# One indirect table fetch, later row transpositions, routing in parts and warm-up products in a fused adapter and mixture-of-experts kernel

## Chip, cores and metric

The kernel runs on one core of one Trainium2 chip. The metric is device time in microseconds (us), the median over several runs of the whole program. A profile is one execution recorded by the hardware profiler; its span goes from the first to the last recorded instruction.

## What is computed

The input x holds 8 sequences of 256 rows with 1024 columns, 2048 rows in all. The reference, cut to its core:

```
w = weight[adapter_ids]                     # per sequence, one of 8 matrices 1024 x 1024
y = einsum('bsi,boi->bso', x, w)            # "cond"
shared = silu(y @ Sg.T) * (y @ Su.T) @ Sd.T # shared expert, inner size 1024
probs  = softmax(y @ gate_w.T)              # 16 experts
top-2, renormalised -> combine              # row by row
e_out  = (silu(y @ Wg[e].T) * (y @ Wu[e].T)) @ Wd[e].T   # inner size 256, per expert
out = x + shared + sum_e combine[:, e] * e_out
```

All is float32. The kernel splits each operand into a high part (a float32r value) and a low part (the remainder), and makes three products per pair: high by high, high by low, low by high.

## The kernel before

**Layout.** Rows are worked in 4 groups of 512 (GT), each of 4 blocks of 128 (NB). Groups 0 and 1 form a first pair and 2 and 3 a second pair for the shared expert.

**Weights.** `load_w` (L89) is the only way by which weights come in: SP issues a 512-KB load to a staging buffer (4 of them), ScalarE casts it to the high part (L80), VectorE subtracts for the low part (L81), both in a buffer `hl` of the pool `whl` (5 of them). After each load it takes one entry from the list `between` and lets that work be queued behind the load's split; this is how other work is strewn among the loads by hand. The order within each engine's queue is fixed when the program is built, by a scheduler that simulates the program and may move an instruction ahead when it finds its data ready; `issue_after` keeps an instruction behind another one on that one's engine.

**Stages.**
1. `cond(b)` (L209) multiplies sequence b by its adapter matrix: 8 weights and 2 loads of transposed x, 96 products of 512 columns (L104 to L106), results to DRAM (`y_d`, L233). The adapter's number is read by SP from `it_sb`.
2. Rows of y come back by POOL's queue (`y_block`, L347), and VectorE transposes them (L178) to the operands `raw` of the shared expert, or to `tt`.
3. The shared expert's up part uses seven half-size products in place of eight (class `Up`, L374): stages A to D for the first pair, each with weights from `sgu` and sums of weights (`sums_b`, L434, which loads two pieces of sgu by L439 and L440 into free parts of S and raw, and stores sums in `ss_d`). Their products are L425, 512 columns each.
4. `route(g, parts)` (L236) makes one group's router logits, 16 or 32 products (L242, from `rb`, the split of transposed rows), then on VectorE the softmax, the top two and each row's rank within its expert. It scatters row numbers and weights to a table in DRAM, `tab_d`, by 8 indirect stores (L333). For groups 1 to 3 its operands come from `parts_of` (L363).
5. After group 3, VectorE orders the experts by load (L782 to L817). `entries` (L660) fetches the table for a list of experts: for each, SP reads the expert's number and issues two small loads, `tb` (L670, for the row numbers) and `cr` (L671, for the weights). `places` transposes tb and adds offsets by four POOL instructions (L656), which gives the gather indices `ix`; `weights` transposes cr on TensorE (L683) and copies it to `cw` (L686). It is called for experts 0 and 1 first, then for the other 14.
6. `expert_rows` (L690) gathers an expert's rows by 8 to 10 indirect loads on POOL (L579); `transpose_rows` (L205) turns and splits them into `yte`. Meanwhile `shared_down` (L533) does the down part of the shared expert for groups 0 and 1, 384 products, adding each finished accumulator to rows of x on VectorE (L554).
7. The 16 experts follow, then the second pair's shared expert with `combine` (L558), which gathers the experts' outputs.

**Helpers at the beginning.** `constants` (L132) makes identity, triangle and index constants on POOL. `tables` (L155) loads the gate and stores an empty table; `zeros` (L168) stores zero rows from SP.

The calls around the change:

```
between[:] = [None, w[0], w[1], lambda: tables(ring), None, w[2], None, w[3]]
cond(2, ys)
...
between[:] = up.rows_work(1)
up.stage_a(0)
up.stage_a(1)
route(1, parts_of([raw[1][:, :, k * 2 * P : (k + 1) * 2 * P] for k in range(2)]))
zeros(ys)
```

Of the kernel before, what the change touches and what calls it, by code (L numbers as in the profile page):

```python
# [17 lines left out]
P = 128  # L18
B, S, H = 8, 256, 1024
T = B * S  # L20
# [3 lines left out]
G = 4  # L24
GT = T // G
# [5 lines left out]
SLOTS = T + CAP  # L31
# [6 lines left out]
def adapter_moe_kernel(ctx: ExitStack, tc: tile.TileContext, xT, x, itok, wc, gate, wgu, wd, sgu, sd, out):  # L38
# [45 lines left out]

    homes, loads, last_gather, marks = [whl], [0], [None], []
# [3 lines left out]
    def load_w(src, parts=1):  # L89
# [3 lines left out]
        for i in range(parts):  # L93
            cs = slice(i * 1024 // parts, (i + 1) * 1024 // parts)
            last_load[0] = nc.sync.dma_start(st[:, cs], src[:, cs])
            end = split(hl[:, 0, cs], hl[:, 1, cs], st[:, cs])
# [5 lines left out]

    def mm3(ps, lhs, rhs, first, last):
        nc.tensor.matmul(ps, lhs[0], rhs[0], start=first, stop=False)  # L104
        nc.tensor.matmul(ps, lhs[0], rhs[1], start=False, stop=False)  # L105
        nc.tensor.matmul(ps, lhs[1], rhs[0], start=False, stop=last)  # L106
# [4 lines left out]
    gpk = cpool.tile([P, NC * 2 * E + P], FR, tag="gpk", name="gpk")  # L111
# [3 lines left out]
    nc.sync.dma_start(it_sb, itok)  # L115

    ident = cpool.tile([2 * E, 2 * E], F32, tag="ident", name="ident")
# [9 lines left out]
    c1, c2 = (t[:, :, 1:2].bitcast(F32).rearrange("p a o -> p (a o)") for t in tid)  # L127
    msum = cpool.tile([P, E], BF, tag="msum", name="msum")
# [3 lines left out]
    def constants(ring):  # L132
        make_identity(nc, ident)
# [3 lines left out]
        nc.gpsimd.memset(ones, 1.0)  # L137
# [30 lines left out]
    def zeros(ys):  # L168
        zr = ys.tile([P, 1024], F32, tag="yr", name="zr")
        nc.gpsimd.memset(zr, 0.0)  # L170
        nc.sync.dma_start(y_d[T // P].rearrange("a p f -> p a f"), zr[:, :].rearrange("p (a f) -> p a f", a=4))
        nc.sync.dma_start(comb_d[T : T + P, :], zr[:, :E])
        nc.sync.dma_start(os_d[ZROW : ZROW + 16, :], zr[:16, :])
# [19 lines left out]
    def pair_work(tb, ys):  # L193
        tv = tt.rearrange("p k (b n) -> p (k b) n", b=4)
        r = [y_block(tb + k, ys) for k in range(2)]
        return tv, [lambda k=k: transpose_to(tv[:, :, k * P : (k + 1) * P], r[k], 4) for k in range(2)]

    def transposed_pair(tb, ys):
        tv, works = pair_work(tb, ys)
        for work in works:  # L200
            work()
        return tv


# [4 lines left out]
    def cond(b, rows):  # L209
        xt = [load_w(xT[b, :, 0, :], 2 if b == 0 else 1)]  # L210
        aid = nc.values_load(it_sb[0:1, b : b + 1], engines=(mybir.EngineType.SP,), min_val=0, max_val=NA - 1)
        yrow = [rows.tile([P, 1024], F32, tag="yrow", name=f"yrow{k}") for k in range(2)]
        for h in range(2):
            ps = [bank() for k in range(2)]
            for q in range(4):
                if h == 0 and q == 1:
                    xt.append(load_w(xT[b, :, 1, :]))
                w = load_w(wc[ds(aid, 1), h * 4 + q].rearrange("a p f -> p (a f)"), 2 if b == 0 and h == 0 and q == 0 else 1)
# [17 lines left out]
    def route(g, parts):  # L236
        lp = psm.tile([P, GT], F32, tag="sm", name="lp")
        n0 = 0
        for get, n in parts:
            for c in range(NC):  # L240
                for l in range(2):
                    nc.tensor.matmul(  # L242
                        lp[:, n0 : n0 + n],
                        gpk[:, c * 2 * E : c * 2 * E + P],
                        get(c)[l],
                        start=(c == 0 and l == 0),
                        stop=(c == NC - 1 and l == 1),
                    )
            n0 += n
# [3 lines left out]
        for k in range(NB):  # L253
            nc.tensor.transpose(lt[:, k, :], ls[: 2 * E, k * P : (k + 1) * P], ident)
# [108 lines left out]
    def parts_of(srcs):  # L363
        for src in srcs:
            t = []
            for k in range(2):
# [618 lines left out]
```

## Time and profile before

| | |
|---|---|
| median of 3 runs | 1003.71 us (998.79 to 1004.02) |
| the profiled execution's own time | 1005.67 us |
| its span | 1003.8 us |
| mean granted TensorE clock | 0.997 |
| instructions | 14185, of them 5043 products |
| moved by DMA | 252.45 MB, mean 251 GB/s |
| largest DMA queues, share of 16 engines | SP 50.5%, POOL 20.7%, ACT 4.6% |

On the page, engines are PE (TensorE's products), PEld (its weight loads), DVE (VectorE), ACT (ScalarE), POOL (GpSimd) and SP (SyncE). In the rows by slices each digit is a fortieth of the span (25 us) in tenths. A row of a timeline gives the start, the duration, the engine, the line, the operation, what is written and read, and in brackets the idle time before it and who ended it. A row of waits gives the total, the number and the longest, in us. In a chain of waits each row is a start, a length and what ran. Stages by time: the eight `cond` blocks, stages A to D and the four routings until about 362 us, `shared_down` for groups 0 and 1 until 457, the experts until 758, the second pair until 998.

### The profile page before, as it was taken

The page shows a single profiled execution, that of the slowest core. Times are in us where ns is not written, and L with a number is a line of the kernel's source. Part 1 is how long each engine was busy: PE and PEld are TensorE (multiplying, and loading weights), DVE is VectorE, ACT ScalarE, POOL GpSimd, SP SyncE. Part 2 cuts the span into 40 slices and gives each one's busy share as a digit, 9 for nine tenths or more (in the row PEclk, how much of TensorE's full clock was granted, in tenths as well). Part 3 has the DMA queues.
Part 4 walks back from the last instruction along what each step waited for, and adds up shares of the span by engine and source line. Part 5 has one row for each costly group of instructions (what it writes and reads, how often), then busy time and mean ns, then how long its engine had stood idle before and what let it go on. Part 6 is the DMA issues. An engine that isn't in the chain of part 4 may idle for free.

```text
span 1003.8 us, 14185 instructions
## 1 busy us (share of the span) xinstructions
PE 980.0 (98%) x5043; PEld 839.8 (84%) x5043; DVE 661.6 (66%) x886; ACT 531.6 (53%) x709; POOL 303.5 (30%) x312
## 2 busy tenths in 40 slices
PE   6989999999999999989999999999999999999997
PEld 5868888888788888869999999999998888888886
DVE  5567588565875886847978878878785324565531
ACT  5546466466563451316777767767665556233220
POOL 1000303000003004847885664650003442503200
PEclk9999999999999999999999999999999999999999
DMA  8988647978768133739988888888878999956931
GB/s 296 319 299 296 210 148 230 389 271 308 283 219 296 44 126 118 268 117 358 332 315 297 269 292 288 278 286 306 283 252 305 260 327 305 290 147 198 263 127 44
DMA packets 83782, 252.45 MB, mean 251 GB/s; under 512 B 13366, under 2 KB 22198, under 8 KB 83702
## 3 DMA queue, kind: packets, MB, share of 16 engines
q1 hardware_dynamic: 51526, 174.07, 50.5%
q0 software_dynamic: 19312, 60.47, 20.7%
q10 hardware_dynamic: 12864, 16.91, 4.6%
q8 instruction: 41, 0.67, 0.3%
q14 instruction: 39, 0.32, 0.1%
HBM read 203.17 MB, written 48.25 MB: 250 GB/s over the span
## 4 chain that ended last, share of the span: by engine, by line
PE 84%; DMA 6%; POOL 3%; issue 3%; DVE 2%; SPq 1%; ACT 1%; ACTq 0%; POOLq 0%; DVEq 0%
PE acc L425 28%; PE acc L105 18%; PE acc L106 18%; PE acc L104 17%; DMA st<-wc 3%; PE acc L647 2%; POOL yg L579 2%; DMA y_d<-yrow 1%; DMA yr<-y_d 1%; PE lp L242 1%; DVE hl L81 1%; POOL tab_d L333 1%; ACT hl L80 1%; DMA st<-xT 1%; SPq L670 0%
## 5 line engine op out<-in xcount | busy, mean ns | idle before, releaser
L81 DVE TENSOR_TENSOR hl<-st,hl 128x1024 fp32r<-128x1024 f32 (+1 forms) x254 | 305.0, 1209 | 176.8 <-ACT hl L80 175.7
L80 ACT CAST hl<-st 128x1024 fp32r<-128x1024 f32 (+1 forms) x254 | 262.9, 1042 | 203.6 <-PE acc L106 80.4
L425 PE MATMUL acc<-op,hl 128*128 128x512 f32 x1056 | 242.6, 390 | 0.5 <-DVE hl L81 0.5
L425 PEld LDWEIGHTS acc<-op,hl 128*128 128x128 f32 x1056 | 197.5, 188 | 41.7 <-DVE hl L81 1.0
L579 POOL DMA_INDIRECT yg<-y_d,ix x128 | 162.7, 1271 | 57.9 <-issue 34.1
L104 PE MATMUL acc<-yte,hl 128*128 128x256 f32 (+6 forms) x512 | 147.4, 288 | 0.0
L106 PE MATMUL acc<-yte,hl 128*128 128x256 f32 (+6 forms) x512 | 147.3, 288 | 0.0
L105 PE MATMUL acc<-yte,hl 128*128 128x256 f32 (+6 forms) x512 | 146.9, 287 | 0.0
L105 PE MATMUL acc<-hl 128*128 128x512 f32 x256 | 101.0, 394 | 2.8 <-DVE hl L81 2.8
L104 PE MATMUL acc<-hl,ht 128*128 128x512 f32 x256 | 99.6, 392 | 1.4 <-DVE acc L554 1.4
L105 PE MATMUL acc<-hl,ht 128*128 128x512 f32 x256 | 100.6, 393 | 0.0
L104 PE MATMUL acc<-hl 128*128 128x512 f32 x256 | 92.1, 395 | 8.6 <-ACT hl L80 8.6
L106 PE MATMUL acc<-hl 128*128 128x512 f32 x256 | 100.4, 392 | 0.0
L106 PE MATMUL acc<-hl,ht 128*128 128x512 f32 x256 | 100.0, 392 | 0.0
L105 PEld LDWEIGHTS acc<-yte,hl 128*128 128x128 f32 x512 | 96.4, 188 | 0.6
L104 PEld LDWEIGHTS acc<-yte,hl 128*128 128x128 f32 x512 | 96.4, 188 | 0.6
L106 PEld LDWEIGHTS acc<-yte,hl 128*128 128x128 f32 x512 | 96.2, 188 | 0.0
L347 POOL DMA_DIRECT2D yr<-y_d x24 | 13.3, 552 | 249.5 <-DMA y_d<-yrow 138.4
L425 PE MATMUL acc<-op,shl 128*128 128x512 f32 x288 | 66.7, 389 | 0.0
L104 PEld LDWEIGHTS acc<-hl 128*128 128x128 f32 x256 | 48.3, 190 | 19.4 <-ACT hl L80 9.5
L425 PEld LDWEIGHTS acc<-op,shl 128*128 128x128 f32 x288 | 54.1, 188 | 11.2
L333 POOL DMA_INDIRECT tab_d<-tid,sli x32 | 35.1, 1098 | 87.7 <-DVE ranks L326 78.9
(191 smaller groups left out, 1330.5 us busy)
## 6 DMA issues: line engine op xcount, KB each, us to landing
st<-wgu SPq DMA_DIRECT2D x64, 512.0 KB
st<-wc SPq DMA_DIRECT2D x63, 512.0 KB
st<-sd SPq DMA_DIRECT2D x32, 512.0 KB
st<-wd SPq DMA_DIRECT2D x32, 512.0 KB
os_d<-o SPq DMA_DIRECT2D x32, 512.0 KB
yr<-y_d POOLq DMA_DIRECT2D x24, 512.0 KB, 6.4
st<-sgu SPq DMA_DIRECT2D x24, 512.0 KB
st<-ss_d SPq DMA_DIRECT2D x20, 512.0 KB
```

Source lines behind the costliest of these rows:

```text
L80: nc.scalar.copy(hi, src)
L81: return nc.vector.tensor_tensor(lo, src, hi.bitcast(F32), op=ALU.subtract).ins
L104: nc.tensor.matmul(ps, lhs[0], rhs[0], start=first, stop=False)
L105: nc.tensor.matmul(ps, lhs[0], rhs[1], start=False, stop=False)
L106: nc.tensor.matmul(ps, lhs[1], rhs[0], start=False, stop=last)
L242: nc.tensor.matmul(lp[:, n0 : n0 + n], gpk[:, c * 2 * E : c * 2 * E + P], get(c)[l], start=(c == 0 and l == 0), stop=(c == NC - 1 and l == 1),
L333: i = nc.gpsimd.indirect_dma_start(out=tab_d[:, :], out_offset=bass.IndirectOffsetOnAxis(ap=sli[:, k : k + 1], axis=0), in_=tid[r][:, tb, ...
L347: nc.gpsimd.dma_start(r, y_d[tb].rearrange("a (i t) f -> (a i) (t f)", t=4))
L425: nc.tensor.matmul(ps, lhs[x], rhs[y], start=(first and c == 0 and i == 0), stop=(c == 3 and i == 2), skip_group_check=True)
L579: last_gather[0] = nc.gpsimd.indirect_dma_start(out=r[:, t * 256 : (t + 1) * 256], out_offset=None, in_=y_d.rearrange("k a p f -> (k a p) f"),
L647: nc.tensor.matmul(ps, a3[:, fi, :], w[fi][:, l, hs], start=(fi == 0 and l == 0), stop=(fi == 1 and l == 1))
```

## The change

**Table.** The table's stride per expert, SLOTS, becomes a multiple of 320 (ENTRIES), so that the first 320 entries of an expert are one row of a view. `entries` no longer loops: VectorE works out on each partition p the row of the expert that is p modulo 16 in the order (`column`, four instructions), one indirect load on POOL fetches these rows to all 128 partitions, one VectorE transposition and one addition give `ix` for all experts. `weights` runs once, held behind the last product queued then.

**Order.** The transpositions of the first expert's rows are queued after loads 4, 6 and 7 of the second `shared_down` (before: 1, 3 and 5). `parts_of` is replaced by `half_part`, and routing is queued through `between` among the loads of stage A (group 1) and of cond 6 and stage C (group 2); group 3 keeps its place. The first loads are issued in a given order (`load_first`), the second half of x one weight later; gate and empty table, and the first two pieces of sgu, are held behind the loads issued by then. `sums` is split into a list of instructions, called in the same place.

**Beginning and end.** Twelve products of constants are queued first on TensorE. `zeros` stores from POOL. The last four output stores go by ACT. `sq` moves from a row buffer of `ys` to `mid`. `G = 4` is renamed GN.

```diff
+ENTRIES = -(-CAP // 32) * 32
+SLOTS = -(-(T + CAP) // ENTRIES) * ENTRIES
...
+    def load_first(xsrc, wsrc):
+        pieces = []
+        for src in (xsrc, wsrc):
+            st = wst.tile([P, 1024], F32, tag="wst", name="st")
+            loads[0] += 1
+            pieces.append((src, st, homes[loads[0] % len(homes)].tile([P, 2, 1024], FR, tag="whl", name="hl")))
+        for k, i in ((0, 0), (1, 0), (1, 1), (0, 1)):
+            src, st, hl = pieces[k]
+            cs = slice(i * 512, i * 512 + 512)
+            with tc.issue_after(last_load[0].ins):
+                last_load[0] = nc.sync.dma_start(st[:, cs], src()[:, cs])
+            split(hl[:, 0, cs], hl[:, 1, cs], st[:, cs])
+        return pieces[0][2], pieces[1][2]
...
+    def after_loads(work):
+        def later():
+            with tc.issue_after(last_load[0].ins):
+                work()
+        return later
...
+    nc.gpsimd.memset(ones, 1.0)
+    warm = psm.tile([P, 4, P], F32, tag="sm", name="warm")
+    for k in range(12):
+        nc.tensor.matmul(warm, ones, ones[:, :].rearrange("p (o n) -> p o n", o=1).to_broadcast([P, 4, P]), start=True, stop=True)
...
-        nc.sync.dma_start(y_d[T // P].rearrange("a p f -> p a f"), zr[:, :].rearrange("p (a f) -> p a f", a=4))
+        nc.gpsimd.dma_start(y_d[T // P].rearrange("a p f -> p a f"), zr[:, :].rearrange("p (a f) -> p a f", a=4))
...
-                if h == 0 and q == 1:
+                if h == 0 and q == 2:
                     xt.append(load_w(xT[b, :, 1, :]))
...
+    def half_part(lp, k, src):
+        t = []
+        for q in range(2):
+            rb = whl.tile([P, 2, 4, 2 * P], FR, tag="whl", name="rb")
+            split(rb[:, 0], rb[:, 1], src[:, 4 * q : 4 * q + 4, :])
+            t.append(rb)
+        route_part(lp, k * 2 * P, lambda c: [t[c // 4][:, l, c % 4, :] for l in range(2)], 2 * P)
+
+    def group_work(lp, g, ys):
+        tv = tt.rearrange("p k (b n) -> p (k b) n", b=4)
+        r = [y_block(g * NB + k, ys) for k in range(2)]
+        def block(k):
+            transpose_to(tv[:, :, k % 2 * P : k % 2 * P + P], r[k], 4)
+            if k < 2:
+                r.append(y_block(g * NB + k + 2, ys))
+        works = []
+        for k in range(2):
+            works += [lambda k=k: block(2 * k), lambda k=k: block(2 * k + 1), lambda k=k: half_part(lp, k, tv)]
+        return works
...
+    def entries(pool, column):
+        cr = pool.tile([P, ENTRIES, 2], F32, tag="cr", name="cr", bufs=1)
+        ib = pool.tile([P, ENTRIES // 32, 32], F32, tag="ib", name="ib", bufs=1)
+        nc.gpsimd.indirect_dma_start(
+            out=cr.rearrange("e s o -> e (s o)").bitcast(I32),
+            out_offset=None,
+            in_=tab_d.rearrange("(e s) o -> e (s o)", s=ENTRIES),
+            in_offset=bass.IndirectOffsetOnAxis(ap=column, axis=0),
+        )
+        nc.vector.transpose(ib, cr[:, :, 0].rearrange("p (t i) -> p t i", i=32))
+        nc.vector.tensor_scalar(ix, ib.rearrange("p t n -> p n t")[:, :E, :].bitcast(I32), seg[:, 0:1], None, op0=ALU.add)
...
-    between[:] = [None, w[0], w[1], lambda: tables(ring), None, w[2], None, w[3]]
+    between[:] = [None, w[0], w[1], after_loads(lambda: tables(ring)), None, w[2], None, w[3]]
...
-    between[:] = up.rows_work(1)
+    w = up.rows_work(1)
+    lp = logits()
+    part = lambda k: lambda: half_part(lp, k, raw[1][:, :, k * 2 * P : (k + 1) * 2 * P])
+    between[:] = [w[0], w[1], w[2], both(w[3], part(0)), part(1), lambda: route(1, lp)]
     up.stage_a(0)
     up.stage_a(1)
-    route(1, parts_of([raw[1][:, :, k * 2 * P : (k + 1) * 2 * P] for k in range(2)]))
+    up.stage_a(2)
     zeros(ys)
-    up.stage_a(2)
+    after_loads(lambda: up.sums_loads(0))()
...
-    between[:] = [None, None, None, w[0], None, None, w[1]]
+    lp2 = logits()
+    w = group_work(lp2, 2, ys)
+    between[:] = [None, None, None, w[0], None, None, w[1], None, None, w[2], both(*w[3:]), lambda: route(2, lp2)]
     cond(6, ys)
-    route(2, parts_of(tv if k == 0 else transposed_pair(2 * NB + k, ys) for k in (0, 2)))
...
-    places, weights = entries(pe[1], [0, 1])
-    places()
+    weights = entries(pe[1], column)
     e0 = expert_rows(pa[1], 0)
-    between[:] = [None] * 4 + [weights]
     shared_down(0, G, ring, down_rows(0, ys), xs_d)
     rs = expert_rows(pa[1], 1)
-    places, weights = entries(pe[1], range(2, E))
     yt, works = expert_yt_work(pa[1], e0)
-    between[:] = [works[0], None, works[1], places, works[2], None, weights]
+    between[:] = [None, weights, None, works[0], None, works[1], works[2]]
     shared_down(1, S_, ring, down_rows(1, ys), xs_d)
```

## Prediction

> **What bounds the kernel now.** I read the page first: its busy row, then the slices.
>
> ```profile
> PE 980.0 (98%) x5043; PEld 839.8 (84%) x5043; DVE 661.6 (66%) x886; ACT 531.6 (53%) x709; POOL 303.5 (30%) x312
> ...
> DMA  8988647978768133739988888888878999956931
> ```
>
> TensorE sets the time, but 98% flatters it. A 512-column product is recorded as lasting 390 ns although the next one starts 227 ns later, so gaps below 0.2 us look busy. I therefore went through TensorE's rows in order of time and took, for each product, the time to the next start less the median for its shape (227 ns at 512 columns, 118 at 256, 139 at 304). The medians sum to 970.5 us. Beside them stand 7.3 us before the first product, 6.7 us after the last start, and 19.3 us beyond the pace; together the span of 1003.8. The 19.3 lie at: 7.3 to 11.7 us, 2.2; 11.7 to 14.2, 1.3; 35, 0.6; 57 to 60, 2.2; 71 to 75, 2.0; 130, 0.9; 266, 2.1; 355 to 380, 0.8; 433, 1.7; 441.8 to 445.2, 3.2; 445.3 to 449, 1.6; scattered, 0.8. From 450 us on, where the experts begin, there is nothing to win. No change that leaves the products alone can go below about 984.5 of span.
>
> The list of TensorE's waits names the releasers:
>
> ```profile
> PE acc L104 <- ACT hl L80: 8.6, 3, 7.3
> PE ct L683 <- DMA cr<-tab_d: 3.0, 1, 3.0
> PE acc L105 <- DVE hl L81: 2.8, 4, 1.4
> PE acc L104 <- DVE acc L554: 1.4, 1, 1.4
> ```
>
> Then TensorE's timeline around the largest ones (start, duration, form), first the beginning:
>
> ```profile
> 10.91 0.63 PE L105 MATMUL acc<-hl 128*128 128x512 f32 x1
> 11.34 0.61 PE L106 MATMUL acc<-hl 128*128 128x512 f32 x1
> ...
> 12.02 0.39 PE L106 MATMUL acc<-hl 128*128 128x512 f32 x1
> 12.61 0.73 PE L104 MATMUL acc<-hl 128*128 128x512 f32 x2 [0.21 <-ACT hl L80]
> 13.87 0.50 PE L105 MATMUL acc<-hl 128*128 128x512 f32 x1 [0.53 <-DVE hl L81]
> 14.21 0.40 PE L106 MATMUL acc<-hl 128*128 128x512 f32 x1
> ```
>
> The first ten products start 0.43 apart, later ones 0.23. But the thirteenth starts at 12.61 because its weight is just cast, the fifteenth at 13.87 because its low part is just made: data, not pace, sets where the second group of twelve begins. And the middle:
>
> ```profile
> 441.77 0.39 PE L104 MATMUL acc<-hl,ht 128*128 128x512 f32 x1
> 445.20 0.43 PE L683 MATMUL ct<-ident,cr 16*128 16x16 f32 x3 [3.04 <-DMA cr<-tab_d]
> 445.56 0.79 PE L105 MATMUL acc<-hl,ht 128*128 128x512 f32 x1
> 446.15 0.63 PE L106 MATMUL acc<-hl,ht 128*128 128x512 f32 x1
> ```
>
> Three small transpositions of table weights stand in TensorE's queue and wait for cr. Their loads are 28 small DMAs (two for each of 14 experts), issued by SP from 431.8 to 444.1, 0.44 us each, and SP began only when POOL had zeroed cr at 431.2, behind the second expert's row gathers. After the gap the pace is halved again. The stretches confirm this (columns: length; busy time and count of PE, PEld, DVE, ACT, POOL; granted clock, DMA share, GB/s):
>
> ```profile
> 7.30:11.70 4.40, 4.37 (x10) 3.42 (x11) 1.74 (x3) 1.85 (x3) 0.00 (x0) 1.00 1.01 329
> 445.20:448.60 3.40, 3.40 (x10) 2.79 (x11) 0.32 (x2) 0.00 (x0) 2.58 (x5) 0.51 0.84 245
> ```
>
> Granted clock 0.51 goes with a 0.43 pace. At the start the row says 1.00 with the same 0.43, so I trust the pace.
>
> **Part by part.**
>
> *One table fetch.* Removed: 32 small DMAs on SP, POOL's zeroing, four POOL additions twice. So the transpositions that wait for cr find it there some 40 us early: 3.2 + 1.6 = 4.8 us. I take 4.6 (bounds 2 and 4.8, the low end if the weight products meet another wait). Added: four VectorE steps for the column, 0.2 us each by the 16-column rows, in a chain that has slack (below), and a POOL fetch of 128 rows of 2,560 B, 328 KB. It must wait for the last table scatter, issued at 393.7 and landed near 396.6, where SP's first table load started before. The nearest rows are the 128-KB row gather (5.3 us from issue to landing) and the 512-KB block read (6.4), so about 5.5. [...] Behind the waiting fetch on POOL stand only those gathers. Behind VectorE's transposition of the fetched table stand splits of weights for up to 5.5 us; ScalarE at that time waited 12.4 us for TensorE to free weight buffers, four loads of 24 products (5.4 us each) ahead, so TensorE doesn't see it.
>
> *Later row transpositions.* The wait at 433 is an accumulator bank whose addition (L554) came late, because VectorE sat before transpositions of rows that hadn't landed. They move behind later loads, using the 30 us of slack: 1.5 (0 to 1.7).
>
> *Constant products.* Twelve, 0.43 apart if slow: from about 1.1 us (their memset goes first on POOL) to 6.2, ahead of the first real one at 7.3, so free. [...] By the timeline a fast array only reaches the wait at 12.61 sooner: nothing by itself.
>
> *Order of the first loads.* What ends that wait is the second weight piece. The change puts it ahead of the second half of x, so 0.5 MB less stands in front: 1.4 us at the 360 GB/s of this stretch. I take 1.3 for both together (0 to 3.4, the two items in full).
>
> *Early loads moved.* SP issued the gate (7.5 us), the empty table (9.5) and two pieces of sgu (11.9, 13.0), and a 0.5-MB store followed at 22.5: 1.9 MB among loads running at 300 GB/s, 6 us of transfer. Sgu goes to about 150 us, where the stretch 140 to 160 has DMA 0.62 busy; gate and table to about 50. The wait at 35 goes (0.6). The one at 57, where ScalarE sat 3.7 us for x, should go too, but a chain then bites:
>
> ```profile
> 57.06 6.40 DMA y_d<-yrow
> ...
> 64.01 6.43 DMA yr<-y_d
> ...
> 71.63 1.19 DVE hl L81
> ```
>
> Store, read back, transposition, and behind it on VectorE the weight split that TensorE needs: 14.6 us from the end of the second block, whatever came before. So most of 2.2 + 2.0 moves from 57 to 71. I take 1.0 (-2 to 3.8), and charge 0.3 (0 to 1.5) for the gate's cast, which now stands in ScalarE's queue with its load issued just before.
>
> *Routing in parts.* The same 112 router products. At 266 TensorE ran into them before their operand was split; now half of them fall among later loads, with stage C's products ready beside them: 1.2 (-1 to 2.1). At 130: 0.4 (-2 to 0.9). Each half takes two of five weight buffers, as before.
>
> *Zeros on POOL, last stores on ACT.* SP waited 16.6 us for POOL's zeros, but its next load (133.9) waited for a buffer anyway; POOL is idle there, three issues at 0.55 us: 0. The last store was issued at 998.3 and landed at 1001.3; another queue changes that by -0.3 to 0.5: 0.
>
> Sum: 4.6 + 1.5 + 1.3 + 0.6 + 1.0 - 0.3 + 1.2 + 0.4 = 10.3. The profiled execution took 1005.7 for its span of 1003.8, so 995.4 for a span of 993.5; from the runs' median, 1003.7, it is 993.4. I say 993.5.
>
> **Rivals.**
>
> *Hidden anyway.* The start is held by the store-and-read chain and the routing waits only move; just the table and transposition parts count, 4.6 + 1.5: 997.6. For it: 14.6 us of chain that the change doesn't touch. Against: DMA share 0.9 to 1.0 until 60.
>
> *A wait in place of the one removed.* The fetch or a moved transposition blocks VectorE until a weight or a bank is late, 4 us, and a gap of over 3 us costs 1.6 more at half clock: about 999. For it: VectorE's queue is in order, and gathers landed late there. Against: the cover of 20 us.
>
> *Slower: router products at the head of TensorE's queue.* In group 1 the first half's split is written behind the fourth transposition, which waits for rows landed at 124.4; ready then at 128.2. If the order of the queues keeps this, TensorE arrives after one stage (106.9 + 48 products of 227 ns = 117.8) and waits 10.4, plus 1.6 for the clock: 12.0, more than all gains, 1005.4; twice, in group 2 as well, 1017. It decides from a wait over 10.3. Against: before, the same split ran at 109.9, ahead of those rows, and 11 router products stood between others without a wait.
>
> That the one fetch isn't made, or not early, is the second rival's limit: without the 4.6 it is 998.
>
> **Numbers.** Forecast 0.60, hidden anyway 0.18, wait replaced 0.12, slower 0.10. About 5 us, 0.5%, is what a measurement can tell here (the three runs span 5.2). Below 998.7 I put 0.58 of the first, 0.12 of the second, 0.03 of the third: 0.73; above 1008.7, 0.07; between, 0.20. The range runs from near the floor (984.5 + 1.9, rounded up to 987) to 1002.
>
> **What would show it.** No TensorE wait on cr, granted clock 1.00 through 440 to 450; first table index before 404; real products 0.23 apart from 7.3 us, the second group complete near 12.5; a wait near 70 still there. Wrong would be: a wait of TensorE on rb or lp over 3 us, VectorE waiting for cr with TensorE idle, or a start that gains over 5 us.

## The result and the profile after

The changed kernel is slower. Its median is 1010.64 us (1009.55 to 1013.2, 4 runs) against 1002.59 us (998.79 to 1004.02, 4 runs) on the same chip: ratio 1.0086, 95% interval 1.006 to 1.0112. Measured again in two later sets of runs, beside before each time, the ratio was 1.0077 (1.0044 to 1.0111) and 1.012 (1.0089 to 1.0152). The forecast was 993.5. Medians are over all executions; ratios leave out those in which the chip was in a slower state, so the two can differ a little.

The profiled execution took 1009.55 us, its span 1007.8. The pair of traces differs by only 4.0 us of span, since the profiled execution of before (1005.67) was slower than all its timed runs and that of after its fastest.

The page of after, the two rows shown of before:

```profile
PE 988.2 (98%) x5052; PEld 844.5 (84%) x5052; DVE 659.2 (65%) x887; ACT 531.3 (53%) x709; POOL 311.1 (31%) x314
...
DMA  7887837989779345587898888888878999956931
```

The busy share is again 98% and says nothing. TensorE's waits in after say more:

```profile
PE acc L127 <- DVE acc L619: 2.8, 1, 2.8
PE acc L127 <- ACT hl L82: 2.6, 1, 2.6
PE lp L269 <- ACT rb L82: 2.3, 1, 2.3
PE lp L269 <- issue: 1.9, 1, 1.9
...
PE acc L486 <- DVE X L569: 1.1, 1, 1.1
```

The wait on cr is gone, as predicted. In its place stand a wait for an accumulator's addition (L619), and one on rb, the operand of the router products. The prediction had named such a wait, if over 3 us, as a sign that it is wrong: here it is 2.3, and 0.8 on the second split of rb; in the two repeats it is 4.8 and 6.0.

I keep the prediction's measure: the start of each product less the median pace of all work before it, TensorE's **lag**. It grows where TensorE loses time. By stretches of TensorE's own work (not of the clock on the wall), in us:

| work done | lost before | lost after | gained | predicted |
|---|---|---|---|---|
| 0 to 60 | 15.3 | 11.9 | 3.4 | 2.6 with the next row |
| 60 to 110 | 0.5 | 4.3 | -3.8 | |
| 110 to 150 (group 1) | 1.3 | 6.7 | -5.4 | 0.4 |
| 150 to 300 (group 2) | 1.9 | 1.3 | 0.7 | 1.2 |
| 300 to 400 | 0.8 | 2.1 | -1.3 | 0 |
| 400 to 430 (table) | 6.4 | 4.6 | 1.8 | 6.1 |
| 430 to 970 | 0.4 | 0.4 | 0 | 0 |

The column of gains adds to -4.7 by its unrounded values; 0.4 of a shorter tail and 0.4 less pace work bring it to the -4.0 of the spans.

**Group 1.** POOL in after (start, duration, instruction, idle before it):

```profile
113.95 0.53 POOL L376 DMA_DIRECT2D yr<-y_d  x1 [19.76 <-DMA y_d<-yrow]
114.81 1.03 POOL L362 DMA_INDIRECT tab_d<-tid,sli  x1 [0.33 <-issue]
...
124.72 0.96 POOL L362 DMA_INDIRECT tab_d<-tid,sli  x1 [0.30 <-issue]
125.68 0.58 POOL L376 DMA_DIRECT2D yr<-y_d  x1
```

and what follows from it on VectorE, ScalarE and TensorE:

```profile
133.61 1.25 DVE L210 STREAM_TRANSPOSE raw<-yr 128x1024 f32<-128x1024 f32 x1 [10.04 <-DMA yr<-y_d]
134.94 1.99 ACT L82 CAST rb<-raw 128x1024 fp32r<-128x1024 f32 x2 [8.47 <-DVE raw L210]
136.04 0.48 PE L269 MATMUL lp<-rb,gpk 128*128 128x256 f32 x1 [2.26 <-ACT rb L82]
137.30 3.27 PEld L269 LDWEIGHTS lp<-rb,gpk 128*128 128x128 f32 x15 [1.07 <-DVE rb L83]
```

The fourth row block's read stands behind all eight table scatters of group 0. Before, it stood behind four:

```profile
120.22 0.58 POOL L347 DMA_DIRECT2D yr<-y_d  x1
...
124.44 1.25 DVE L178 STREAM_TRANSPOSE raw<-yr 128x1024 f32<-128x1024 f32 x1 [4.90 <-DMA yr<-y_d]
```

In after it is issued at 125.68 and lands 7.9 us later, and everything from the transposition to TensorE waits for it in turn. Of the 9.2 us by which the transposition starts later than before, 5.5 are the place in POOL's queue. The other 3.7 are the landing, which took 4.2 us before; why it takes longer isn't settled.

**The beginning.** TensorE in after:

```profile
9.30 0.39 PE L129 MATMUL acc<-hl 128*128 128x512 f32 x1
12.33 0.73 PE L127 MATMUL acc<-hl 128*128 128x512 f32 x2 [2.65 <-ACT hl L82]
13.59 0.80 PE L128 MATMUL acc<-hl 128*128 128x512 f32 x1 [0.53 <-DVE hl L83]
14.18 0.63 PE L129 MATMUL acc<-hl 128*128 128x512 f32 x1
...
16.73 0.39 PE L127 MATMUL acc<-hl 128*128 128x512 f32 x1
```

The first twelve products run 0.23 apart almost at once, and the last of them starts 2.7 us earlier than before (9.30, not 12.02). Then TensorE has nothing for 2.65 us, and from 13.59 the pace is 0.43. The stretches of after (length; busy time and count of PE, PEld, DVE, ACT, POOL; granted clock, DMA share, GB/s) agree, with a clock of 0.50 and then 1.00:

```profile
13.60:16.70 3.10, 3.10 (x7) 2.50 (x8) 2.38 (x2) 1.89 (x2) 0.00 (x0) 0.50 0.84 258
16.70:20.00 3.30, 3.30 (x16) 2.67 (x15) 1.78 (x2) 1.25 (x2) 0.00 (x0) 1.00 0.96 330
```

**The table.** VectorE in after, from the fetch's result to the addition:

```profile
412.35 0.51 DVE L736 STREAM_TRANSPOSE ib<-cr 128x320 f32<-128x320 f32 x1 [5.89 <-DMA cr<-tab_d,column]
...
439.66 1.25 DVE L210 STREAM_TRANSPOSE tt<-yg 128x1024 f32<-128x1024 f32 x1 [0.66 <-DMA yg<-y_d,ix]
441.93 0.68 DVE L619 TENSOR_TENSOR acc<-acc,acc 128x512 f32<-128x512 f32 x1
```

and TensorE behind it:

```profile
442.67 0.50 PE L127 MATMUL acc<-hl,ht 128*128 128x512 f32 x1 [2.79 <-DVE acc L619]
...
443.55 0.63 PE L127 MATMUL acc<-hl,ht 128*128 128x512 f32 x1
443.98 0.63 PE L128 MATMUL acc<-hl,ht 128*128 128x512 f32 x1
```

The last scatter ended 8.4 us later than before. The fetch was issued at 408.26, another 5.2 us behind it, and the first gather started at 414.45 (before: 401.94). Of these 12.5 us, 8.4 are the later scatters and 4.2 the longer way from the last scatter to the first gather. So the row transpositions came later too, and stood ahead of the addition that frees an accumulator. TensorE waited 2.79 us for it, and went on 0.43 apart.

The block transposed at 439.66 is the second expert's, whose gathers begin on POOL behind the first expert's ten:

```profile
427.10 1.84 POOL L644 DMA_INDIRECT yl<-y_d,ix  x1 [0.30 <-issue]
429.24 1.23 POOL L644 DMA_INDIRECT yg<-y_d,ix  x1 [0.30 <-issue]
```

So it was before: the transposition ahead of the late addition there, at 432.94, waits for gathers issued from 425.17 on, while the first expert's ten had ended by 419.1.

```profile
432.94 1.25 DVE L178 STREAM_TRANSPOSE tt<-yg 128x1024 f32<-128x1024 f32 x1 [0.56 <-DMA yg<-y_d,ix]
434.11 0.65 DVE L554 TENSOR_TENSOR acc<-acc,acc 128x512 f32<-128x512 f32 x1
434.82 0.50 PE L104 MATMUL acc<-hl,ht 128*128 128x512 f32 x1 [1.40 <-DVE acc L554]
```

The change moves the first expert's transpositions only.

### The profile page after: what moved, and what is told of

The parts are those of the page before. It is cut to its first block, busy times and chain, and to the rows that moved or that the text cites. A ratio compares the mean times of both kernels' runs of the same rounds, so it can differ in the third digit from the quotient of the medians.

```text
span 1007.8 us, 14050 instructions
## 1 busy us (share of the span) xinstructions
PE 988.2 (98%) x5052; PEld 844.5 (84%) x5052; DVE 659.2 (65%) x887; ACT 531.3 (53%) x709; POOL 311.1 (31%) x314
## 4 chain that ended last, share of the span: by engine, by line
PE 87%; DMA 5%; POOL 2%; issue 2%; DVE 1%; ACT 1%; SPq 0%; DVEq 0%; POOLq 0%; ACTq 0%
PE acc L486 25%; PE acc L128 20%; PE acc L129 20%; PE acc L127 19%; DMA y_d<-yrow 2%; PE acc L712 2%; PE lp L269 2%; POOL yg L644 1%; POOL tab_d L362 1%; DMA yr<-y_d 1%; DMA st<-wc 1%; DMA raw<-sgu 1%; DMA yg<-y_d,ix 1%; DVE hl L83 1%; DMA acc<-x 1%
## 5 line engine op out<-in xcount | busy, mean ns | idle before, releaser
L82 ACT CAST hl<-st 128x1024 fp32r<-128x1024 f32 (+1 forms) x254 | 263.0, 1042 | 171.3 <-PE acc L129 82.0
L644 POOL DMA_INDIRECT yg<-y_d,ix x128 | 158.6, 1239 | 63.7 <-issue 37.2
L362 POOL DMA_INDIRECT tab_d<-tid,sli x32 | 39.8, 1244 | 142.7 <-DVE ranks L355 108.2
```

The costliest lines, as they stand in the source:

```text
L82: nc.scalar.copy(hi, src)
L362: i = nc.gpsimd.indirect_dma_start(out=tab_d[:, :], out_offset=bass.IndirectOffsetOnAxis(ap=sli[:, k : k + 1], axis=0), in_=tid[r][:, tb, ...
L644: last_gather[0] = nc.gpsimd.indirect_dma_start(out=r[:, t * 256 : (t + 1) * 256], out_offset=None, in_=y_d.rearrange("k a p f -> (k a p) f"),
```

## Experiments

Eighteen runs in five sets; the runs of a set share a chip and its runs of the kernel before. In all sets but the fourth the chip took 1027 to 1032 us for the kernel before itself. There every trace loses 11 to 30 us between 400 and 450 us of work (last section), so ratios are taken within a set only, and the lag of those sets is read mainly up to there. "Start" is the lag at 10 us of work; the other columns are losses.

| kernel | median, us | before there | ratio (95%) | start | 60-110 | 110-125 |
|---|---|---|---|---|---|---|
| before, first trace | 1002.59 | | | 10.8 | 0.5 | 1.2 |
| after, first trace | 1010.64 | 1002.59 | 1.0086 (1.006-1.0112) | 12.0 | 4.3 | 6.6 |
| sgu_late | 1034.82 | 1026.58 | 1.0082 (1.0052-1.0113) | 9.8 | 3.0 | 1.5 |
| y3_first | 1027.79 | 1026.58 | 1.005 (1.002-1.008) | 12.1 | 3.7 | 0.0 |
| route1_back | 1045.04 | 1026.58 | 1.0245 (1.0145-1.0346) | 11.7 | 4.0 | 12.5 |
| table_back | 1047.06 | 1026.58 | 1.0218 (1.0146-1.029) | 13.1 | 4.9 | 10.1 |
| after_again | 1037.88 | 1030.14 | 1.0077 (1.0044-1.0111) | 9.3 | 3.2 | 8.5 |
| fetch_only | 1039.31 | 1030.14 | 1.0118 (1.001-1.0227) | 11.0 | 0.6 | 2.4 |
| y3_sgu | 1035.27 | 1030.14 | 1.0077 (1.0048-1.0107) | 10.3 | 3.7 | 0.0 |
| best1 | 1035.39 | 1030.14 | 1.0106 (1.0006-1.0205) | 9.8 | 5.3 | 0.4 |
| before_again | 1029.61 | 1027.12 | 1.0037 (1.0007-1.0068) | 11.1 | 0.5 | 1.5 |
| y3_e1 | 1021.62 | 1027.12 | 0.9962 (0.9933-0.9991) | 13.7 | 4.8 | 0.0 |
| start_back | 1027.54 | 1027.12 | 1.0032 (0.9999-1.0065) | 11.0 | 0.7 | 9.7 |
| zeros_sp | 1029.39 | 1027.12 | 1.0045 (1.0017-1.0073) | 11.6 | 2.3 | 8.8 |
| after_third | 1016.76 | 1003.34 | 1.012 (1.0089-1.0152) | 12.0 | 3.4 | 9.2 |
| y3_e1_second | 1005.96 | 1003.34 | 1.0033 (1.0015-1.0052) | 12.1 | 4.9 | 0.1 |
| y3_start | 1006.95 | 1003.34 | 1.0031 (1.0015-1.0046) | 11.1 | 1.1 | 0.0 |
| y3_e1_start | 1002.43 | 1003.34 | 0.9997 (0.998-1.0015) | 10.9 | 0.9 | 0.0 |
| best2 | 1028.88 | 1031.81 | 0.9967 (0.9943-0.999) | 10.8 | 2.7 | 0.0 |
| best2_table_back | 1038.13 | 1031.81 | 1.0043 (1.0012-1.0075) | 10.9 | 0.7 | 0.0 |

The kernel before against itself (before_again) gave 1.0037, with an interval that leaves out 1. So differences of 0.4% count for nothing here unless a second run or the trace bears them out.

### Row group 1: why the fourth block came late

**y3_first**: group 0's scatters queue on POOL behind the fourth block's read.

```diff
-    route(0, lp)
+    route(0, lp, scatters)
...
+    def after_read():
+        with tc.issue_after(last_read[0]):
+            scatters[0]()
-    between[:] = [w[0], w[1], w[2], both(w[3], part(0)), part(1), lambda: route(1, lp)]
+    between[:] = [w[0], both(w[1], after_read), w[2], both(w[3], part(0)), part(1), lambda: route(1, lp)]
```

> The changed kernel with group 0's eight table scatters held on POOL behind the read-back of group 1's fourth block; nothing else is moved. Theory A: the read is issued at about 122, as soon as its buffer is free, 3.5 us earlier, and TensorE's lag between 115 and 125 us of work falls from 6.6 to about 3; time 3 to 4 us below the changed kernel. Theory B: lag stays above 5, time within 1 us of the changed kernel.

Its loss there is nil. POOL, VectorE and TensorE in y3_first:

```profile
118.72 0.53 POOL L386 DMA_DIRECT2D yr<-y_d  x1 [26.54 <-DMA y_d<-yrow]
119.95 0.53 POOL L386 DMA_DIRECT2D yr<-y_d  x1 [0.71 <-DMA y_d<-yrow]
120.81 1.03 POOL L367 DMA_INDIRECT tab_d<-tid,sli  x1 [0.33 <-issue]
...
124.84 1.23 DVE L210 STREAM_TRANSPOSE raw<-yr 128x1024 f32<-128x1024 f32 x1
...
133.93 1.92 PE L269 MATMUL lp<-rb,gpk 128*128 128x256 f32 x15
```

Third and fourth block are read 1.2 us apart, the transposition starts 8.8 us earlier than in after, and the last 15 router products wait for nothing. Over all runs below: the seven traces in which the read stands behind eight scatters lose 6.6 to 12.5 us at 110 to 125 us of work, the nine in which the scatters are held lose 0.0 to 0.4.

**route1_back**: the routing of group 1 in one piece behind stage A(1), as before.

```diff
-    between[:] = [w[0], w[1], w[2], both(w[3], part(0)), part(1), lambda: route(1, lp)]
+    between[:] = w
     up.stage_a(0)
     up.stage_a(1)
-    up.stage_a(2)
+    both(part(0), part(1))()
+    route(1, lp)
     zeros(ys)
+    up.stage_a(2)
```

> The changed kernel with group 1's routing in its old place: four transpositions among the loads, both halves of the router products after the second step of stage A, zero rows before the third. Theory A: POOL's order of reads and scatters and the sgu loads are as in the changed kernel, so TensorE's lag between 115 and 125 us of work stays at 5 or more; time within 1 us of the changed kernel. Theory B: the lag falls to about 1, as before the change, and the time falls by 4 to 5 us.

It loses 12.5 us there (four runs only, and 6.6 us more at 150 to 200): POOL still issues the fourth read behind eight scatters, at 129.09, and TensorE waits 8.31 us for rb at 139.01. So the parts are not to blame: the place of the products in TensorE's order decides only how long TensorE stands.

**sgu_late**: the two sgu pieces held behind the loads of cond(4).

```diff
-    after_loads(lambda: up.sums_loads(0))()
     up.stage_a(3)
     cond(4, ys)
+    after_loads(lambda: up.sums_loads(0))()
```

> The changed kernel with the two held pieces of sgu loaded one step later, behind the loads of the fifth adapter block. Theory A (group 1's routing waits because its last block of rows is read back late: the sgu pieces delay the third block's read by 2.2 us, and with it POOL's queue order puts the fourth read behind eight table scatters): the fourth read is issued near 120 instead of 125.7, VectorE's wait for it falls from 10.0 to about 5 us, TensorE's lag between 115 and 125 us of work falls from 6.6 to 2 or less; time 4 to 5 us below the changed kernel. Theory B (the router products' new place among the loads is what makes TensorE wait): the lag there stays at 5 or more and the time changes by less than 1 us. For the block order at the beginning both expect no difference.

The loss falls to 1.5, but 6.7 us come back at 150 to 200 us of work, and the ratio stays. Besides, the fourth read moved by itself to behind four scatters (116.24), so this run does not price sgu's traffic alone. It is the only one of the single edits in which it moved: where the scheduler puts the scatters depends on the place of the two pieces.

**zeros_sp**: the zeros on SP's queue again (`nc.gpsimd.dma_start` to `nc.sync.dma_start`, three lines).

> The changed kernel with the three stores of zeros on SP's queue again, in the same place. Theory (the late read of the last block comes mostly from the scatters ahead of it, and the stores of zeros, queued behind the read, only share its bandwidth): the read's landing is 1 to 3 us earlier and the loss at 110 to 125 us of work is 3 to 6 us instead of 6 to 8; 0 to 3 us below the changed kernel. Rival (the zeros are the cause): the loss falls under 2 us.

The loss is 8.8, of which 1.9 are another wait (at 126.09, between products of stage A), so 6.9 beside the 6.6 to 9.2 of the three traces of after; the read lands 7.0 us after its issue. The zeros are not the cause, and what their place on POOL costs is too small to be seen here.

**after_again** and **after_third**, the changed kernel without an edit:

> The changed kernel itself once more, as the control for the others of this job: 1.004 to 1.013 of the kernel before, with TensorE's lp products of the second group waiting over 3 us for rb near 136 us and a loss of 5 to 7 us against its own work between 110 and 125 us of work. If the slower time belonged to one placement of the program or to one chip, it would come out within 0.5% of the kernel before.

> The changed kernel once more as the control of this job: 1.003 to 1.010 of the kernel before, a loss of 6 to 9 us at 110 to 125 us of TensorE's work.

Both as the theory had it.

**y3_sgu**: y3_first and sgu_late together (both diffs).

> The changed kernel with the first group's eight scatters queued on GpSimd behind the fourth block's read, and the sgu pieces behind the loads of the fourth condition. Theory (the second group's loss is the late read of the last block, made late by the scatters ahead of it on GpSimd's queue): the block is there 5 us earlier or more, rb's wait at 136 us is gone, 5 to 6 us below the changed kernel, about 0.996 of it and 1.002 to 1.004 of the kernel before. Rival (the loss is in the routing's place in the order of TensorE): the wait moves to another product and the time stays within 2 us of the changed kernel.

The wait on rb is gone, the ratio is that of after_again to the digit. In its trace between 165 and 232 us VectorE waits for the late pieces:

```profile
DVE S L518 <- DMA S<-sgu: 5.2, 2, 4.7
```

TensorE then waits 3.3 us for a weight made of them (`acc L496 <- ACT shl L82`), and 6.3 us are lost at 150 to 200 us of work. In the traces the gain is there, and given back.

### The table

**table_back**: `entries` of before and its calls in the changed kernel.

```diff
-    weights = entries(pe[1], column)
+    places, weights = entries(pe[1], [0, 1])
+    places()
...
+    places, weights = entries(pe[1], range(2, E))
-    between[:] = [None, weights, None, works[0], None, works[1], works[2]]
+    between[:] = [works[0], None, works[1], places, works[2], None, weights]
```

> The changed kernel with the old table code: small loads of SP, for experts 0 and 1 and then for the other 14, and the old places of the transpositions. Theory C (the one fetch gains as forecast and only part of it is lost to a late accumulator): TensorE waits for cr near 440 to 450 again, 3 us plus 1.6 at half clock, and loses 6.5 us between 410 and 430 us of work where the changed kernel loses 4.7; time 1.5 to 2.5 us above the changed kernel. Rival D (the fetch's chain on POOL and VectorE is what costs): the time is equal or lower by up to 3 us, with no VectorE wait of 5.9 us for cr.

The wait on cr is back (2.4) and the time is far above before, but group 1 lost 10.1 in this execution too, so its ratio doesn't price the table.

**fetch_only**: the kernel before with the fetch and its order of row transpositions (the two parts of that diff the other way, with the column and identity that it needs).

> The kernel before with one part of the change alone: the table entries by one replicated fetch, with its later row transpositions. Theory (the part is good by itself, and in the changed kernel its gain is mostly lost since the gathers start 12 us later there and shared_down's addition stands behind row transpositions): the loss of TensorE in the table's stretch, 6.5 us in the kernel before between 410 and 430 us of work, falls to 1 to 3 us, so 3 to 5 us below the kernel before, ratio 0.995 to 0.997. Rival (the fetch's chain, scatter landing plus issue plus fetch, is what costs): the loss stays at 5 us or more and the ratio at 0.999 to 1.003.

Neither theory: 1.0118 with an interval of 0.022. The trace shows 4.0 us lost at 300 to 320 us of work, which before doesn't have, and a stall beyond 410 (last section) that hides the rest. Inconclusive.

**y3_e1** and **y3_e1_second**: y3_first, with VectorE's transpositions of the second expert's rows held behind the additions of the first half of shared_down(1).

```diff
+                if n == 0:
+                    first_sum[0] = end
...
-    nxt = expert_yt(py[1], rs)
+    with tc.issue_after(first_sum[0]):
+        nxt = expert_yt(py[1], rs)
```

> The changed kernel with two edits: the first group's eight scatters queued on GpSimd behind the fourth block's read (the sgu pieces stay where the change has them), and VectorE's row transpositions of the second expert held behind the additions of the first half of shared_down. Theory (the two losses of the changed kernel are these two orders, and each can be taken away alone): no loss at 110 to 125 us of work, and the addition to the accumulator no longer waited for at 410 to 425, together 7 to 10 us below the changed kernel, 0.996 to 1.001 of the kernel before. Rival (holding the rows only moves the wait to the first expert's operand or the gathers' buffers): 1.003 to 1.006 of the kernel before, as with the scatters alone.

> The version with the scatters behind the fourth block's read and the second expert's row transpositions behind the additions, a second time. If its gain is real it is 0.993 to 0.999 of the kernel before and 8 to 12 us below the changed kernel; if the first measurement was a lucky placement, 1.000 or more of the kernel before.

The first came out at 0.9962, the second at 1.0033: 10.8 us below the changed kernel beside it, but not below before. VectorE, and TensorE behind it, in y3_e1_second:

```profile
436.90 2.48 DVE L629 TENSOR_TENSOR acc<-acc,acc 128x512 f32<-128x512 f32 x4
439.30 2.36 DVE L210 STREAM_TRANSPOSE tt<-yg 128x1024 f32<-128x1024 f32 x2
...
437.64 0.51 PE L127 MATMUL acc<-hl,ht 128*128 128x512 f32 x1 [1.92 <-DVE acc L629]
```

All four additions run in one piece ahead of the second expert's rows. Over the stretch from 400 to 430 us of work TensorE loses 2.2 us, against 4.9 in after_third on the same chip. A wait of 1.9 us for the addition stays: what stands ahead of it on VectorE now are the first expert's transpositions and splits of weights.

**best2_table_back** beside **best2** (below): the same kernel with and without the fetch, the diff of table_back.

> The version before this one with the table entries read as in the kernel before: strips of two experts, then of all, and transpositions waiting for them. It prices the fetch in a kernel without the other losses. Theory (the replicated fetch and the later row transpositions are worth something by themselves, though less than the 6.1 us of the prediction): the loss of TensorE between 390 and 450 us of work is 2 to 5 us larger than with the fetch, and the time as much longer. Rival (the fetch's chain costs what the strips' waits cost): within 1 us of the version with the fetch.

9.3 us longer by the medians (1038.13 and 1028.88), 7.8 by the ratios, the intervals apart. At 380 to 410 us of work it lost 11.1, best2 4.1. The fetch is worth something where nothing takes its gain; how much of this is the stall of the last section, which follows at 440, isn't settled.

### The beginning

**start_back**: no constant products, the first loads in the old order.

```diff
-    for k in range(12):
-        nc.tensor.matmul(warm, ones, ones[:, :].rearrange("p (o n) -> p o n", o=1).to_broadcast([P, 4, P]), start=True, stop=True)
...
-            x0, w0 = load_first(lambda: xT[b, :, 0, :], lambda: weights(0))
+        xt = [load_w(xT[b, :, 0, :], 2 if b == 0 else 1)]
-                if h == 0 and q == 2:
+                if h == 0 and q == 1:
```

The last two lines hold for every cond block, not the first alone: with the new start, the second half of x comes one weight later in all eight.

> The changed kernel with the start of the kernel before: no twelve constant products, the loads of the first condition in their old order. Theory (the start gains by itself, but most of it ends in the row block's store, read and transposition at 75 us): TensorE's lag at 48 to 60 us of work is 2 to 4 us larger than in the changed kernel, and at 80 us of work 0 to 2 us larger; the time is the same to 2 us above the changed kernel. Rival (the start costs, by the pause at 9 to 12 us and the half clock after it): the lag at 80 is lower than in the changed kernel and the time 1 to 3 us below it.

**y3_start**: y3_first and start_back. **y3_e1_start**: y3_e1 and start_back.

> The changed kernel with the scatters behind the fourth block's read and the start of the kernel before (no constant products, old load order). Theory (the late read is the whole loss of the second group, the new start is worth nothing): no loss at 110 to 125 us of work, lag at 10 us of work between 10.8 and 11.1, and 0.998 to 1.002 of the kernel before, that is 5 to 8 us below the changed kernel. Rival (the new start is worth its 1 to 3 us): 1.001 to 1.004 of the kernel before.

> The version before this one with the second expert's row transpositions held behind the additions as well. Theory (the row transpositions ahead of the accumulator's addition cost 4 us, the start nothing): 3 to 6 us below the version before it, and within 2 us of the version with the new start, 0.993 to 0.998 of the kernel before. Rival (holding the rows gains nothing by itself): within 1.5 us of the version before it.

On one chip: 1005.96 with the new start (y3_e1_second), 1002.43 with the old one (y3_e1_start). By these medians the new start costs 3.5 us; the two intervals meet at 1.0015, and the difference is under the 0.4% above, so it needs the traces. The lag at 10 us of work is 10.8 to 11.1 in all eight traces with the old start, and 9.3 to 13.7 (mean 11.5) in the twelve with the new one. TensorE in y3_start:

```profile
11.46 0.40 PE L131 MATMUL acc<-hl 128*128 128x512 f32 x1
12.92 0.73 PE L129 MATMUL acc<-hl 128*128 128x512 f32 x2 [1.07 <-ACT hl L82]
14.18 0.50 PE L130 MATMUL acc<-hl 128*128 128x512 f32 x1 [0.53 <-DVE hl L83]
14.52 0.39 PE L131 MATMUL acc<-hl 128*128 128x512 f32 x1
```

The second weight is ready at 12.92, just 0.6 us later than in after. TensorE, 0.43 apart at first here (8.55 to 10.25), starts its twelfth product at 11.46 and waits 1.07; its pace stays at 0.23. So the new start gains nothing by itself: at 60 us of work the lag is 11.5 in the mean of the twelve traces with it, and 11.7 in that of the five with the old start and the later gate and table (sgu is early again in best2 and best2_table_back). Between 60 and 110, the new start then loses 2.3 to 5.3 us and the old one 0.5 to 2.7. At 110, the lag is 15.4 (12.3 to 19.2) in the mean of the twelve, 12.9 (12.0 to 14.3) of the five, and 14.3 (13.2 to 15.8) of before, before_again and fetch_only. So the new start loses about 2.5, behind the beginning and not in it, and the moved loads gain about 1.4, a mean of few traces whose ranges overlap. Products, order of the first loads and place of x in the later blocks were not tried apart, so which of them costs the 2.5 is open.

**y3_e1_start against y3_start**: 1002.43 and 1006.95, so holding the rows is worth 4.5 us by the medians; their traces lost 4.1 and 4.7 at 400 to 430, so one execution of each doesn't show it (that of y3_e1_start took 1009.45, far above its median).

### Other edits

**best1**: y3_sgu, y3_e1's hold, the table's transposition behind the row arithmetic, and group 0's split and router products spread among the loads of cond(3).

```diff
-    up.begin()
-    route_part(lp, 0, lambda c: chunk(up.b11 if c < 4 else up.b21, c % 4), GT)
-    route(0, lp)
+    between[:] = [None, None, up.begin, None,
+        lambda: route_part(lp, 0, lambda c: chunk(up.b11 if c < 4 else up.b21, c % 4), GT),
+        None, lambda: route(0, lp, scatters)]
```

> The version before this one with two more edits: the first group's split and router products spread among the loads of the fourth condition, so that TensorE has other products while the last row block is stored, read and transposed (a loss of 3.8 us in the changed kernel, 60 to 70 us of work); and VectorE's row transpositions held behind the last addition of the first half of shared_down (a loss of 4.7 us, 410 to 425 us of work). Theory: the three losses add, so 10 to 14 us below the changed kernel, 0.993 to 0.998 of the kernel before. Rival (the same latencies, each moved to the next product): 3 us or less below the version with the scatters and the sgu pieces held, that is 0.999 to 1.004 of the kernel before.

The trace speaks for the rival: 5.3 us are lost at 60 to 110, where after_again lost 3.2 and y3_sgu 3.7. The ratio, from four runs, is too wide to decide (1.0006 to 1.0205).

**best2**: y3_e1_start with the sgu pieces where before has them (`if u:` ahead of `self.sums_loads(u)` and the held call taken out).

> The version with the scatters behind the fourth block's read, the second expert's row transpositions behind the additions and the start of the kernel before, and one edit more: the first two sgu pieces are no longer held behind other loads, as in the kernel before, which has them within its first 16 us. Theory (held, they land late for VectorE's subtraction, which waits 9 to 11 us for them, and TensorE loses 1 to 6 us at 150 to 200 us of work): that loss is gone, as in the kernel before, and the time is 1 to 4 us below the version with the pieces held, 0.996 to 0.999 of the kernel before. Rival (1 MB more among the first loads costs as much at 28 to 60 us of work, where the kernel before lost up to 3.9 us): the same as the version with the pieces held, 0.999 to 1.002.

The ratio is 0.9967, the lowest but the first y3_e1's 0.9962, but 2.8 us are still lost at 150 to 200, between the 1.2 and 6.4 of the two traces with held pieces. The theory of the edit isn't shown. Besides, the two lowest ratios come from chips with the stall, and their traces lost 10.7 (y3_e1) and 19 (best2) at 400 to 450, against 27.6 in before_again on the chip of y3_e1; so a shorter stall may be part of them. With y3_e1 once at 0.9962 and once at 1.0033, and before against itself at 1.0037, no version here is shown to be faster than the kernel before; y3_e1_start is level with it and 14.3 us faster than the changed kernel beside it.

**before_again**, the kernel before itself:

> The kernel before itself, with a trace of this job's chip. On it the changed kernel and its variants lost 18 to 30 us in the stretch from 400 to 450 us of TensorE's work, where all engines show waits for nothing that the profile shows, and up to 7 us more at 700 to 800; the profile of before on its first chip lost 6.4 there. If that belongs to the chip and not to the change, the kernel before shows it too: a loss of 15 to 30 us between 400 and 450 and a span of 1018 to 1036 us. If it came with the change, the kernel before keeps a loss of 6 to 8 us there and a span near 1004 us.

It lost 27.6 us between 400 and 450 on that chip, so that stall is not the change's.

## Why the prediction was wrong

- **At 130: 0.4 (-2 to 0.9).** Measured -5.4, and 6.6 to 9.2 lost in the three traces of after. This is the step that failed most. It costed where the router products stand on TensorE and left out which queue their operand comes through. In POOL's queue the scatters of group 0, unchanged, moved ahead of the read, which was issued at 125.68, as the eighth of them ended (in y3_first, ahead of them, at 119.95): 5.5 us by their place, and 3.7 more by a slower landing. The rival "router products at the head" had the waiting instruction right, on the second half instead of the first, at 6.6 to 9.2 instead of 12.0; and "decides from a wait over 10.3" was wrong because the gains were not 10.3.
- **Constant products and load order: 1.3 (0 to 3.4).** Measured about -2.5. The prediction saw that a fast array "only reaches the wait sooner"; it missed that the wait grew to 2.65 us and that the pace after it fell again (0.43 from 13.59 to 16.7, granted clock 0.50), so that nothing was left of the start at 60 us of work. It also put nothing down for the x loads of the later blocks, which the change moves too. The loss itself comes at 60 to 110; its cause is open.
- **Early loads moved: 0.6 + 1.0.** About 1.4, near the forecast in size. A wait at 70 to 80 stayed, as foreseen. "Sgu goes to about 150 us" was wrong: SP issued it at 107, held only behind loads issued by then.
- **Routing at 266: 1.2.** Before lost 2.0 at 240 to 260, after 0.1: 1.9, with 1.3 lost again at 330 to a new wait on X (L569).
- **Table fetch 4.6, later row transpositions 1.5.** The wait on cr went with its 4.8 us, yet 1.8 in all came. The second term had the wrong rows: the transposition ahead of the late addition was the second expert's, before and after, and the change moves the first expert's. It turned to about -2.9: 4.6 us are lost where before lost 1.7 besides cr, by gathers 12.5 us later, 2.79 us of waiting and the 0.43 pace after it (443.55 to 446.54). The 30 us of slack, in the trace of before from the end of the first expert's operand at 427.9 to its first product at 457.8, were TensorE's for the first expert's rows, not VectorE's for the accumulator. The fetch itself took 4.1 us from issue to landing, less than the prediction's 5.5, but it was issued 6.2 us after the last scatter, where the prediction had 2.9.
- **Zeros on POOL: 0.** "POOL is idle there" is wrong, it was in the scatters until 125.7; but the zeros cost nothing that zeros_sp could tell.

## What to carry to other kernels

When a consumer is moved, follow its operand back through every queue that issues a part of it, and list what else the scheduler can now put ahead of the load: here eight unmoved scatters cost 6.6 to 9.2 us, and all that the change gained in its first trace is 5.9. An engine that is made to start earlier is worth only what its data allow, and a longer pause can cost its clock: here the twelfth real product started 2.7 us earlier, the thirteenth 0.3 (12.33, not 12.61), and after the pause of 2.65 us the granted clock was 0.50 for 3.1. Before moving work out of another's way, make sure that it is the work in the way: here the second expert's rows were, and the first expert's were moved.

## What the runs showed of the hardware

- A pause of TensorE of 2.65 us (after), 2.57 (y3_first) or 2.37 (after_third) was followed by a 0.43 pace for about 3 us, one of 1.23 (after_again) or 1.07 (y3_start) by 0.23. Between them length alone doesn't decide: 1.85 us in after, before 77.05, was followed by 0.43 from 78.36 on, 1.92 in y3_e1_second, before 437.64, by 0.23. The fall didn't come with the first product: after the 2.65 us three products started within 1.3 us (granted clock 0.88 from 12.3 to 13.6), then the pace was 0.43 (0.50 to 16.7).
- On four of the chips every trace, that of the kernel before too (27.6 in before_again), lost 11 to 30 us between 400 and 450 us of work, for the most part in stretches in which TensorE, ScalarE and VectorE stood or crawled while POOL issued gathers. A stretch of before_again, its columns as in the stretches of after:

```profile
470.00:480.00 10.00, 2.47 (x6) 1.44 (x5) 0.00 (x0) 0.00 (x0) 5.72 (x7) 0.50 0.49 156
```

Six products in 10 us, nothing on VectorE and ScalarE. From 440 to 490 TensorE's waits are put down to "issue" for 15.2 us, 3.1 go to cr and 0.3 to an addition; of ScalarE's, 24.1 us are put down to "remote", 16.0 to loads of weights. Neither name stands for work that the profile shows. The cause is open.
